# Layer 3 of a four-layer kernel: its preparation dealt out anew between the engines, and bn asked for earlier in each scan step

## The chip, the cores and the metric

The kernel runs on one core of one Trainium2 chip, as one launch. The metric is device time in microseconds (us). The kernel before was run three times; the profile is of one further execution. Engines are called as in the profile: PE (TensorE; PEld are its weight loads), DVE (VectorE), ACT (ScalarE), POOL (GpSimd) and SP (SyncE, which here issues the DMAs).

## What is computed

Four layers are applied in turn to four images of 256 channels and 64 x 64 pixels, each as x + layer(groupnorm(x)): a deformable convolution, an attention, a second deformable operation (DCNv4), and a Mamba block. Only the last is touched. With L = 4096 pixels as a sequence, 512 inner channels d and 16 states n:

```python
xz = einsum('bld,ed->ble', xs, in_proj_w);  u, res = split(xz, 2)
u = silu(depthwise_conv(u, conv_w, taps=4, causal) + conv_b)
dt, B, C = split(einsum('bld,ed->ble', u, x_proj_w), [16, 32])
delta = softplus(einsum('blr,dr->bld', dt, dt_proj_w) + dt_proj_b)
state[l] = exp(delta[l] * A) * state[l-1] + delta[l] * B[l] * u[l]     # for each d and n, along l
y[l] = sum over n of state[l] * C[l]
out = einsum('ble,de->bld', (y + u * D) * silu(res), out_proj_w)
```

## The kernel before: staging, order and names

The four images go one after the other, each through the layers 0 to 3. Layer 3 (`layer3`, L1081) cuts the 4096 pixels into 8 chunks of 512 columns. The 512 inner channels are four blocks of 128 partitions, called `dc` in the code. For each chunk the 16 states are 16 *steps*, so an image has 128 steps, s = 16 j + n for chunk j and state n.

**One step** (the loop at the end of `layer3`): DVE forms h = du * bn for four blocks (L1537). `bn` is row n of B, spread over all partitions by a matmul with `pick` (`state`, L1460), in a PSUM pool of one bank. For the states in `helped` (14, 15, 0 to 5) DVE forms only three blocks, and POOL the fourth from a row that a DMA has spread (`quarter`, L1468, `bs`). Then four scans: ACT makes da = exp(delta * A) into one of two PSUM banks (L1547), DVE runs the recurrence (L1548). Scans 0 and 1 come ahead of the middle of the step, scans 2 and 3 after it. POOL saves the last column (L1560) and multiplies by C (L1563, `cn`, also spread by a DMA). PE adds h into the four `y` banks two steps later (`add`, L1438; in a chunk's first add also u * D, L1436). At n=2 DVE multiplies the previous chunk's y by silu(res) (`gated`, L1514).

**The front.** While chunk j-1 is scanned, chunk j is prepared in *slots* of these steps, written out by hand in `front(j)`: each entry has a step, a half (0 between scans 1 and 2, 1 after scan 3, -1 and 2 at the start and the end of the step), a PE part and a rest. In order: normalise x (`begin`), four projections (L1242), four convolutions, each of four tap matmuls with diagonal weights (L1285), silu of u and of the previous chunk's gates between two table loads (`silu`, L1299, L1258), the projection to dt, B and C (`shares` L1309, `keep` L1313, and its DMA to `cd`), dt to delta (`step`, L1324, L1330, L1331), softplus in six wide operations of ACT and POOL (L1337 to L1357), the cast of B into two bf16 parts (`split`, L1369 to L1377) and four gate projections. A front's step 0 lies `LEAD` = 4 steps ahead of its predecessor's n=0 (2 for j=1). `close(j)` projects the finished chunk back and adds x (L1396, L1400), in two groups, and issues the output DMA; `fetch` loads the next image's x into the columns that became free, `count` takes its statistics on DVE (L152).

All front matmuls share one PSUM bank, so each waits until ACT has copied the one before. `fill(s, half)` issues the first PE part of a slot ahead of time, `empty` the rests. The order of the engines' queues is the order of these calls (a manual schedule): on PE in step s the part of (s,1), then `state(s + 1)`, the y adds of step s-2 and the part of (s+1,0).

**Chunk 0** has no predecessor: `first` (L1130) prepares it, and part of chunk 1, ahead of the loop. It projects four blocks (L1152). Blocks 1 and 3 are convolved by DVE (L1159, L1161), blocks 0 and 2 by PE (L1177). POOL normalises chunk 1 (L1169) and casts `pick` (L1110). After the silus (L1178, L1179), the projection (L1181), its copy `dbc` (L1184) and the dt matmuls (L1190) come the first three projections of chunk 1 and the four gate projections (L1198), and then a softplus block by block: Abs, Exp, Relu and Ln on ACT (L1220, L1221, L1222, L1215), four operations on DVE (L1223, L1224, L1216, L1217), and one subtraction (L1227) and the cast of B (L1209, L1211, L1212) on POOL. `state(0)` follows `first`; slot (0,0) then holds the fourth projection of chunk 1, and slots (0,0) and (1,0) the copies of the gates (L1492).

Of the kernel before, what the change touches and what calls it, by code (L numbers as in the profile page):

```python
# [16 lines left out]
P = 128  # L17
# [46 lines left out]
class Net:  # L64
# [1016 lines left out]
    def layer3(self, x, out, nxt, early):  # L1081
# [5 lines left out]

        nc, tc = self.nc, self.tc
        C = 512
        NC, LEAD = N // C, 4  # L1090
        with (
# [18 lines left out]
            nc.gpsimd.tensor_copy(pick.rearrange("p n m -> p (n m)"), rows.rearrange("p a b -> p (a b)"))  # L1110
# [9 lines left out]
            kept = pa.tile([P, 2, C], F32, tag="kept", name="kept")  # L1120
# [9 lines left out]
            def first():  # L1130
# [23 lines left out]
                for dc in range(4):  # L1154
                    pu = spare()
                    project(pu, xn, dc)
                    if dc % 2:
                        nc.vector.tensor_copy(up[:, dc, 3:], pu)
                        nc.vector.tensor_scalar_mul(u[:, dc, :], up[:, dc, :C], cw[:, dc, 0:1])  # L1159
                        for i in range(1, 4):  # L1160
                            nc.vector.scalar_tensor_tensor(  # L1161
                                u[:, dc, :], up[:, dc, i : i + C], cw[:, dc, i : i + 1], u[:, dc, :], ALU.mult, ALU.add
                            )
                    else:
                        nc.scalar.copy(up[:, dc, 3:], pu)
                for ct in range(2):
                    if ct == 0:
                        c1["xn"] = pa.tile([P, 2, C], F32, tag="xn3", name="xn3")
                    nc.gpsimd.tensor_scalar(  # L1169
                        c1["xn"][:, ct, :], x[:, ct, C : 2 * C], rs[:, ct : ct + 1], shift[:, ct : ct + 1], ALU.mult, ALU.add  # L1170
                    )
                nc.gpsimd.tensor_copy(tail, up[:, :, C : C + 3])
                px = bank()
                for dc in (0, 2):
                    cv = spare()
                    for i in range(4):
                        nc.tensor.matmul(cv, conv[:, dc, i, :], up[:, dc, i : i + C], start=(i == 0), stop=(i == 3))  # L1177
                    nc.scalar.activation(u[:, dc + 1, :], u[:, dc + 1, :], AF.Silu, bias=cb[:, dc + 1 : dc + 2])  # L1178
                    nc.scalar.activation(u[:, dc, :], cv, AF.Silu, bias=cb[:, dc : dc + 1])  # L1179
                for k, dc in enumerate((1, 3, 0, 2)):  # L1180
                    nc.tensor.matmul(px, xpw[:, dc, :], u[:, dc, :], start=(k == 0), stop=(k == 3))  # L1181
# [17 lines left out]

                c["gates"] = [spare() for _ in range(4)]  # L1200
                for dc, pg in enumerate(c["gates"]):
                    project(pg, xn, 4 + dc)
# [5 lines left out]
                def split(lo, hi):  # L1208
                    nc.gpsimd.tensor_copy(bp[lo:hi], dbc[lo:hi])  # L1209
                    if hi < P:  # L1210
                        nc.gpsimd.tensor_copy(t[hi:], dbc[hi:])  # L1211
                        nc.gpsimd.tensor_sub(dbc[hi:], dbc[hi:], t[hi:])  # L1212

                def end(dc):
                    nc.scalar.activation(w[:, dc, :], w[:, dc, :], AF.Ln)  # L1215
                    nc.vector.tensor_add(delta[:, dc, :], delta[:, dc, :], w[:, dc, :])  # L1216
                    nc.vector.tensor_mul(du[:, dc, :], delta[:, dc, :], u[:, dc, :])  # L1217

                for dc in range(4):
                    nc.scalar.activation(w[:, dc, :], pzs[dc], AF.Abs, bias=dtb[:, dc : dc + 1])  # L1220
                    nc.scalar.activation(du[:, dc, :], w[:, dc, :], AF.Exp, scale=-1.0)  # L1221
                    nc.scalar.activation(delta[:, dc, :], pzs[dc], AF.Relu, bias=dtb[:, dc : dc + 1])  # L1222
                    nc.vector.tensor_scalar_add(w[:, dc, :], du[:, dc, :], 1.0)  # L1223
                    nc.vector.scalar_tensor_tensor(  # L1224
                        du[:, dc, :], w[:, dc, :], -1.0, du[:, dc, :], ALU.add, ALU.subtract
                    )
                    nc.gpsimd.tensor_sub(delta[:, dc, :], delta[:, dc, :], du[:, dc, :])  # L1227
                    if dc < 3:
                        split(*((0, 64), (64, 96), (96, 128))[dc])
                    if dc:  # L1230
                        end(dc - 1)
                end(3)
                for dc in range(3):
                    nc.scalar.copy(c1["up"][:, dc, 3:], pus[dc])

# [24 lines left out]
            def front(j):  # L1260
# [17 lines left out]
                for dc in range(4):  # L1278
                    put((dc + 1) // 2, (dc + 1) % 2, *project(j, dc, lambda dc=dc: c["up"][:, dc, 3:]))

                def convolve(dc):
# [7 lines left out]
                    def rest():  # L1289
                        nc.scalar.activation(c["u"][:, dc, :], c["b"], AF.Identity, bias=cb[:, dc : dc + 1])  # L1290
                        if dc == 0:
                            nc.gpsimd.tensor_copy(tail, c["up"][:, :, C : C + 3])
# [3 lines left out]
                for dc in range(4):  # L1296
                    put(2 + dc, 1, *convolve(dc))
# [5 lines left out]
                put(6, 0, None, silu)  # L1303
# [14 lines left out]
                put(7, 1, shares, keep)  # L1318
# [16 lines left out]
                for dc in range(4):  # L1335
                    put(8 + dc // 2, dc % 2, *step(dc))
                put(10, 0, None, lambda: nc.scalar.activation(c["du"], c["du"], AF.Exp, scale=-1.0))  # L1337

                def one():
                    c["w"] = pa.tile([P, 4, C], F32, tag="w3", name="w3")  # L1340
                    nc.scalar.activation(c["w"], c["du"], AF.Identity, bias=self.ones[:, 0:1])

                put(10, 1, None, one)


                put(10, 2, None, lambda: nc.gpsimd.tensor_add(c["delta"], c["delta"], c["du"]))
                put(
                    12,
                    0,
                    None,  # L1350
                    lambda: nc.scalar.activation(c["du"], c["w"], AF.Identity, bias=self.ones[:, 0:1], scale=-1.0),
                )
                put(13, 0, None, lambda: nc.scalar.activation(c["w"], c["w"], AF.Ln))
                last = 17 if j > 1 else 15
                put(13, 2, None, lambda: nc.gpsimd.tensor_add(c["delta"], c["delta"], c["du"]))
                put((13 + last) // 2, 2, None, lambda: nc.gpsimd.tensor_add(c["delta"], c["delta"], c["w"]))
                put(last, 2, None, lambda: nc.gpsimd.tensor_mul(c["du"], c["delta"], c["u"]))  # L1357

                for dc in range(4):
                    at = ((14, 0), (14, 1), (15, 0), (15, 1)) if j > 1 else ((10, 1), (11, 0), (11, 1), (12, 1))  # L1360
                    put(*at[dc], *gate(j, dc))
# [19 lines left out]
                for i in range(3):  # L1381
                    put((11, 12, 14)[i], i % 2, None, split(i))
                return todo

            def close(j):
# [5 lines left out]
                def project(ot):  # L1391
                    def pe():
# [6 lines left out]
                        xs = kept[:, ot, :] if last else x[:, ot, bass.ts(j, C)]  # L1399
                        nc.tensor.matmul(c["b"], self.ident, xs, start=False, stop=True)  # L1400

                    def rest():
                        to = kept if last else x[:, :, bass.ts(j, C)]
# [5 lines left out]
                for ot in range(2):  # L1409
                    todo.append((11 + 2 * ot - LEAD, 1, *project(ot)))  # L1410
                if not last:
                    todo.append((15 - LEAD, -1, None, lambda: fetch(j)))

                    todo.append((13 - LEAD + DS if j < NC - 2 else 17 - LEAD, -1, None, lambda: count(j)))
# [12 lines left out]
            def keep():  # L1427
                for ct in range(2):
# [33 lines left out]
            def quarter(s):  # L1462

                if s < NC * DS:
                    c = chunks[s // DS]
                    hs[s] = pb.tile([P, 4, C], F32, tag="h", name="h", bufs=4)
                    if s % DS in helped:
                        nc.gpsimd.tensor_mul(hs[s][:, 3:4, :], c["du"][:, 3:4, :], c.pop(("bs", s % DS)))  # L1468


            slots = {}
            for j in range(1, NC):
                for step, half, pe, rest in front(j):
                    at = DS * (j - 1) - (LEAD if j > 1 else 2) + step
# [10 lines left out]
            for i in range(2):  # L1485
# [8 lines left out]
                slots.setdefault((i, 0), []).append((None, gates))  # L1494

# [20 lines left out]
            with tc.manual_schedule(  # L1516
# [10 lines left out]
                state(0)  # L1527
# [4 lines left out]
                for s in range(total):  # L1532
                    j, n = s // DS, s % DS
                    c = chunks[j]
                    h = hs.pop(s)
                    d = 3 if n in helped else 4
                    nc.vector.tensor_mul(  # L1537
                        h[:, :d, :], c["du"][:, :d, :], c.pop(("bn", n)).to_broadcast([P, d, C])
                    )
# [5 lines left out]
                    def scan(dc):  # L1545
                        da = pda.tile([P, C], F32, tag="da", name="da")
                        nc.scalar.activation(da, c["delta"][:, dc, :], AF.Exp, scale=al[:, dc, n : n + 1])  # L1547
                        nc.vector.tensor_tensor_scan(  # L1548
                            h[:, dc, :], da, h[:, dc, :], carry[:, dc, n : n + 1], ALU.mult, ALU.add
# [4 lines left out]
                    quarter(s + 1)  # L1554
                    empty(s, 0)
# [12 lines left out]
                    state(s + 1)  # L1568
# [134 lines left out]
```

## Time and profile before

| | us |
|---|---|
| median of three runs (lowest, highest) | 9831.43 (9831.18, 9837.31) |
| the profiled execution | 9825.3 |
| its span, first to last instruction | 9823.5 |
| busy in the span: PE, DVE, ACT, POOL | 8552.6, 7522.1, 4893.9, 7112.0 |
| image 0, layer 3: `shift` known | 1523.0 |
| first product, second product | 1563.7, 1570.2 |
| product of step 16 | 1683.0 |
| last scan ends | 2500.1 |

The other images begin layer 3 at 3963.8, 6388.5 and 8824.5 and take 40.5 to 41.7 from `shift` to the first product and 928 to 937 from there to the last scan's end. From the product to the last scan of image 0 the costliest groups are the scans (L1548, 512 of them, 617.3 busy), POOL's product with C (L1563, 127 that were recorded, 574.9), the y adds (L1438, 471.2), da (L1547, 346.9) and the product (L1537, 255.7).

A row of the timeline has the start, the duration from the first to the last of the merged instructions, the engine, the line, the operation with the program's names (output, then inputs), the shape, the count, and in brackets how long the engine had been idle and what ended that. A row of the waits has the total, the number of waits and the longest. A float32 matmul counts as two passes of PE, so four matmuls stand as x8.

### The profile page before, as it was taken

Reading aid. Unit: us, or ns where it says so; the run is one execution under the profiler, and the core shown is the slowest. Engines: PE = TensorE matmul, PEld = TensorE weight load, DVE = VectorE, ACT = ScalarE, POOL = GpSimd, SP = SyncE. Lnnn points to the kernel's source line nnn. Section 1 sums busy time; section 2 is a strip of 40 time slices with the busy share of each in tenths; the row PEclk is TensorE's granted clock in tenths of the full one; section 3 lists DMA queues with packets and bytes.
Section 4 is the critical chain, followed back from the end, with each engine's and each line's share of the span. In section 5 each row is a group of like instructions: output and inputs, shape, how many; then the busy total and the mean of one; then the engine's idle time right before and its main releaser. Section 6 shows DMA issues by size and latency. Waiting matters only on the chain. (4 is left out here: it accounts for less than half of the span.)

```text
span 9823.5 us, 89566 instructions
## 1 busy us (share of the span) xinstructions
PE 8552.6 (87%) x29129; PEld 4208.7 (43%) x29129; DVE 7522.1 (77%) x8175; ACT 4893.9 (50%) x7532; POOL 7112.0 (72%) x4220
## 2 busy tenths in 40 slices
PE   5789998998778999899878899989987889998997
PEld 3643343333464344333346434433334643443333
DVE  4764498999676459899968645989996764689998
ACT  3753335665474333566547433266655733326664
POOL 3746687888474668798857467789985746778997
PEclk9999999999899999999989999999998999999999
DMA  7840011222783001122279201122228820111221
GB/s 255 319 158 1 26 50 56 64 62 67 257 320 139 1 30 47 58 63 63 67 272 333 107 1 35 51 57 62 62 64 313 324 73 1 39 51 55 60 60 51
DMA packets 415274, 1024.78 MB, mean 104 GB/s; under 512 B 38771, under 2 KB 111916, under 8 KB 412748
## 3 DMA queue, kind: packets, MB, share of 16 engines
q0 software_dynamic: 165888, 604.05, 17.0%
q1 hardware_dynamic: 248908, 414.90, 13.7%
q8 instruction: 233, 3.82, 0.2%
q14 instruction: 245, 2.01, 0.1%
HBM read 851.70 MB, written 93.37 MB: 96 GB/s over the span
## 5 line engine op out<-in xcount | busy, mean ns | idle before, releaser
L1548 DVE TENSOR_TENSOR_SCAN h<-da,carry,h 128x512 f32<-128x512 f32 x2048 | 2469.0, 1264 | 138.3 <-ACT da L1547 78.0
L1563 POOL TENSOR_TENSOR h<-h,cn 128x2048 f32<-128x2048 f32 x508 | 2299.7, 4527 | 41.3 <-POOL carry L1560 0.8
L1547 ACT ACTIVATE da<-delta,l3a 128x512 f32<-128x512 f32 x2048 | 1393.1, 689 | 1064.1 <-DVE h L1548 1061.5
L1438 PE MATMUL y<-h,ident 128*128 128x512 f32 x4096 | 1907.6, 610 | 12.4 <-POOL h L1563 12.4
L344 POOL DMA_INDIRECT g<-tab,idx x1152 | 1359.8, 1180 | 748.6 <-issue 367.5
L565 POOL TENSOR_TENSOR acc<-acc,e 128x1024 f32<-128x1024 f32 x480 | 1126.0, 2346 | 539.5 <-ACT e L561 517.6
L388 PE MATMUL pz<-cols,l0w 128*128 128x256 f32 x4608 | 1211.3, 409 | 184.6 <-DVE cols L377 73.9
L1438 PEld LDWEIGHTS y<-h,ident 128*128 128x128 f32 x4096 | 801.7, 196 | 1251.6 <-issue 1166.7
L353 DVE SCALAR_TENSOR_TENSOR r<-g,wx,r 128x512 f32<-128x512 f32 x1152 | 858.4, 745 | 373.4 <-ACT r L352 251.4
L462 DVE TENSOR_REDUCE m<-pm 128x3 f32<-128x1536 f32 (+2 forms) x340 | 599.5, 1763 | 699.9 <-PE pm L452 699.9
L1537 DVE TENSOR_TENSOR h<-du,bn 128x2048 f32<-128x2048 f32 (+1 forms) x512 | 1022.8, 1998 | 49.9 <-PE bn L1460 49.8
L388 PEld LDWEIGHTS pz<-cols,l0w 128*128 128x128 f32 x4608 | 893.2, 204 | 353.7 <-DVE cols L377 110.4
L561 ACT ACTIVATE e<-sc 128x1024 f32<-128x1024 f32 x512 | 496.1, 1020 | 1029.5 <-PE sc L548 1029.5
L572 PE MATMUL cx<-e,v 128*128 128x512 f32 x2048 | 1001.0, 616 | 0.0
L845 DVE TENSOR_TENSOR prod<-ring,A 128x1280 f32<-128x1280 f32 x640 | 922.4, 1480 | 77.9 <-DMA ring<-ring 60.2
L352 ACT ACTIVATE r<-g,wx 128x512 f32<-128x512 f32 x1152 | 826.5, 717 | 265.0 <-DMA g<-tab,idx 211.6
L862 PE MATMUL pacc<-prod,ident 128*128 128x512 f32 x1920 | 914.5, 611 | 32.8 <-DVE prod L845 21.8
L854 POOL TENSOR_TENSOR prod<-prod 128x512 f32<-128x512 f32 x640 | 801.2, 1277 | 182.2 <-DVE prod L845 157.3
L370 PE MATMUL pt<-ident,acc 128*128 128x128 f32 x2304 | 428.3, 293 | 295.0 <-DVE acc L361 234.2
L572 PEld LDWEIGHTS cx<-e,v 128*128 128x128 f32 x2048 | 352.4, 189 | 599.3 <-issue 596.8
L360 ACT ACTIVATE acc<-r,wy 128x256 f32<-128x256 f32 x1152 | 571.3, 496 | 16.5 <-DVE r L353 13.7
L361 DVE SCALAR_TENSOR_TENSOR acc<-r,wy,acc 128x256 f32<-128x256 f32 x1152 | 548.6, 477 | 0.0
(255 smaller groups left out, 10767.4 us busy)
## 6 DMA issues: line engine op xcount, KB each, us to landing
cn<-cd SPq DMA_DIRECT2D x512, 256.0 KB
tab<-vt SPq DMA_DIRECT2D x112, 640.0 KB
bs<-cd SPq DMA_DIRECT2D x256, 256.0 KB
ring<-ring SPq DMA_DIRECT2D x288, 126.0 KB
ring<-ring SPq DMA_DIRECT2D x288, 124.0 KB
g<-tab,idx POOLq DMA_INDIRECT x1152
x<-in_x SPq DMA_DIRECT2D x64, 256.0 KB
out<-x SPq DMA_DIRECT2D x56, 256.0 KB
```

Source lines behind the costliest of these rows:

```text
L344: nc.gpsimd.indirect_dma_start(out=g[:], out_offset=None, in_=tab[:, :], in_offset=bass.IndirectOffsetOnAxis(ap=idx[:, t, k : k + 1], axis=0),
L353: nc.vector.scalar_tensor_tensor(r, g[:, :, 1, :], wx[:, 1, t, k : k + 1], r, ALU.mult, ALU.add)
L388: nc.tensor.matmul(sums[m][:, ot, :256], wf[:, i, bass.ts(ot, P)], cols[m][:, i, :], start=(i == 0), stop=(i == 17),)
L565: nc.gpsimd.tensor_add(b["acc"], b["acc"], e)
L572: nc.tensor.matmul(blocks[qb]["cx"], v[:, 4 * (i + kt // 4 * 4) + kt % 4, :], e[:, bass.ts(i % 2, 512)], start=(kt == 0 and i == 0), stop= ...
L845: nc.vector.tensor_mul(d["prod"][:, :, t, :].rearrange("p x (g c) -> p x g c", c=GC), ring[y // VR % 4][:, :, y % VR, :].rearrange("p x (g ...
L862: nc.tensor.matmul(d["pd"], self.ident, prod[:, wx, :], start=(wy == 0 and wx == 4), stop=(wy == WIN - 1 and wx == 2),)
L1438: nc.tensor.matmul(c["ys"][dc], self.ident, h[:, dc, :], start=False, stop=(n == DS - 1))
L1537: nc.vector.tensor_mul(h[:, :d, :], c["du"][:, :d, :], c.pop(("bn", n)).to_broadcast([P, d, C]))
L1547: nc.scalar.activation(da, c["delta"][:, dc, :], AF.Exp, scale=al[:, dc, n : n + 1])
L1548: nc.vector.tensor_tensor_scan(h[:, dc, :], da, h[:, dc, :], carry[:, dc, n : n + 1], ALU.mult, ALU.add)
L1563: nc.gpsimd.tensor_mul(h, h, cn.to_broadcast([P, 4, C]))
```

## The change

All of it lies in `layer3`. `first`: blocks go in the order 1, 3, 0, 2; DVE convolves 1, 3 and 0, PE only 2; the cast of `pick` and the normalisation of chunk 1 move from POOL to ACT, as do the casts of B (the subtraction between them stays on POOL), each a block later; Relu and Ln write back into the PSUM bank, and DVE makes the subtraction that POOL had. `state(0)` and then the gate projections stand at the end of `first`.

The loop: `state(s + 1)` moves to the middle of the step, ahead of `fill(s, 1)`. `product` is a function; in the steps of `visits` (those with silu and table loads) the product of the next step is issued in the middle of the step. POOL's quarter has a tile of its own, `hq`. Within a slot the entries with a PE part go first.

The slots: `LEAD` is 5 (3 for j=1). As seen from the scan, with j > 1: projections 0 to 2 and convolutions 0 and 1 come one step earlier, projection 3 one step and a half later, and convolutions 2 and 3 stay; the silus, `keep` and dt stay; the casts of B go to n=6, 7 and 10 and Exp stays at n=6, the two wide Identity operations to the first half of n=7 and the second half of n=8, Ln to the second half of n=9, the gates to n=9 and 10; `close` to n=6 and 8 (from 7 and 9), `fetch` to n=10, and `count` from n=9 to the middle of n=2 of the same chunk. Slot (0,0) holds the first convolution of chunk 1. `kept` shares the buffer of `xn3`.

```diff
-        NC, LEAD = N // C, 4
+        NC, LEAD = N // C, 5
...
-                for dc in range(4):
+                c1["xn"] = pa.tile([P, 2, C], F32, tag="xn3", name="xn3")
+                for dc in (1, 3, 0, 2):
                     pu = spare()
                     project(pu, xn, dc)
-                    if dc % 2:
+                    if dc == 1:
                         nc.vector.tensor_copy(up[:, dc, 3:], pu)
+                    else:
+                        nc.scalar.copy(up[:, dc, 3:], pu)
+                    if dc != 2:
                         nc.vector.tensor_scalar_mul(u[:, dc, :], up[:, dc, :C], cw[:, dc, 0:1])
...
+                    if dc == 3:
+                        nc.scalar.copy(pick.rearrange("p n m -> p (n m)"), rows.rearrange("p a b -> p (a b)"))
...
-                c["gates"] = [spare() for _ in range(4)]
-                for dc, pg in enumerate(c["gates"]):
-                    project(pg, xn, 4 + dc)
...
                 def split(lo, hi):
-                    nc.gpsimd.tensor_copy(bp[lo:hi], dbc[lo:hi])
+                    nc.scalar.copy(bp[lo:hi], dbc[lo:hi])
                     if hi < P:
-                        nc.gpsimd.tensor_copy(t[hi:], dbc[hi:])
+                        nc.scalar.copy(t[hi:], dbc[hi:])
                         nc.gpsimd.tensor_sub(dbc[hi:], dbc[hi:], t[hi:])
                 def end(dc):
-                    nc.scalar.activation(w[:, dc, :], w[:, dc, :], AF.Ln)
-                    nc.vector.tensor_add(delta[:, dc, :], delta[:, dc, :], w[:, dc, :])
+                    nc.scalar.activation(pzs[dc], w[:, dc, :], AF.Ln)
+                    nc.vector.tensor_add(delta[:, dc, :], pzs[dc], delta[:, dc, :])
...
-                    nc.gpsimd.tensor_sub(delta[:, dc, :], delta[:, dc, :], du[:, dc, :])
-                    if dc < 3:
-                        split(*((0, 64), (64, 96), (96, 128))[dc])
+                    nc.vector.tensor_sub(delta[:, dc, :], pzs[dc], du[:, dc, :])
                     if dc:
                         end(dc - 1)
+                        split(*((0, 64), (64, 96), (96, 128))[dc - 1])
                 end(3)
                 for dc in range(3):
                     nc.scalar.copy(c1["up"][:, dc, 3:], pus[dc])
+                state(0)
+                c["gates"] = [spare() for _ in range(4)]
+                for dc, pg in enumerate(c["gates"]):
+                    project(pg, xn, 4 + dc)
...
-                    put((dc + 1) // 2, (dc + 1) % 2, *project(j, dc, lambda dc=dc: c["up"][:, dc, 3:]))
+                    at = ((0, 1), (1, 0), (1, 1), (4, 1))[dc]
+                    put(*at, *project(j, dc, lambda dc=dc: c["up"][:, dc, 3:]))
...
-                    put(2 + dc, 1, *convolve(dc))
+                    at = ((2, 1) if j > 1 else (3, 0), (3, 1), (5, 1), (6, 1))[dc]
+                    put(*at, *convolve(dc))
...
-                    todo.append((11 + 2 * ot - LEAD, 1, *project(ot)))
+                    todo.append((6 + 2 * ot, 1, *project(ot)))
...
+            def product(s):
+                if s not in hs:
+                    c, n = chunks[s // DS], s % DS
+                    h = hs[s] = pb.tile([P, 4, C], F32, tag="h", name="h", bufs=4)
+                    d = 3 if n in helped else 4
+                    nc.vector.tensor_mul(h[:, :d, :], c["du"][:, :d, :], c.pop(("bn", n)).to_broadcast([P, d, C]))
...
+            for todo in slots.values():
+                todo.sort(key=lambda part: part[0] is None)
...
                     scan(0)
                     scan(1)
                     quarter(s + 1)
+                    state(s + 1)
+                    if s in visits:
+                        product(s + 1)
                     empty(s, 0)
                     fill(s, 1)
                     scan(2)
                     scan(3)
                     empty(s, 1)
...
                     empty(s, 2)
-                    state(s + 1)
                     late.append((j, n, h))
```

## The prediction, made before the changed kernel ran

> **What bounds the kernel now.** I read the page's busy shares first, then the table by stage of the first image's layer 3, then VectorE's waits there, then the timeline of single steps. Times are microseconds of the profiled execution; a step is one pass of the scan loop, D is the start of its product (L1537), n its number within a chunk of 16.
>
> The stage table (length, busy time of PE, PEld, DVE, ACT, POOL, clock) of the preparation, of chunk 0 and of one later chunk:
>
> ```profile
> 1522.98:1563.67 40.69, 37.19 (x81) 15.68 (x81) 26.37 (x30) 19.43 (x31) 24.11 (x30) 0.95 0.12 41
> 1563.67:1683.00 119.33, 100.43 (x230) 41.85 (x231) 108.19 (x82) 75.92 (x106) 97.54 (x47) 0.99 0.16 47
> ...
> 1821.68:1939.18 117.50, 107.17 (x254) 45.70 (x253) 111.55 (x87) 74.25 (x103) 105.49 (x48) 1.00 0.22 62
> ```
>
> A chunk of 117.5 is VectorE's (111.6 busy), but TensorE has 107.2 and GpSimd 105.5: three engines within 10% of the end. Whatever holds one of them back a few us is seen. VectorE's waits in this layer (total, times, longest):
>
> ```profile
> DVE h L1548 <- ACT da L1547: 19.6, 16, 4.4
> DVE h L1537 <- PE bn L1460: 12.3, 22, 1.0
> ...
> DVE h L1548 <- POOL h L1468: 2.6, 1, 2.6
> ```
>
> From step 16 on (1683 to 2500) the same view has 14.1 for da and 10.9 for bn: 25.0 an image. The first is the silu visit at n=2 (two table loads, two 2048-wide silus, 6.32 from the first load to the next da), the second TensorE's conv steps, 7.09 against VectorE's 6.56.
>
> The timeline of step 0 shows how close behind the preparation the rest stands:
>
> ```profile
> 1559.66 0.38 PE L1460 MATMUL bn<-bp,pickn 128*128 128x512 bf16 x1 [0.21 <-POOL bp L1209]
> ...
> 1561.34 1.98 PE L1242 MATMUL front<-xn,l3a 128*128 128x512 f32 x4 [1.31 <-ACT up L1234]
> ...
> 1563.38 0.60 ACT L1246 COPY up<-front 128x512 f32<-128x512 f32 x1
> 1563.67 1.75 DVE L1537 TENSOR_TENSOR h<-du,bn 128x1536 f32<-128x1536 f32 x1
> ...
> 1570.24 1.73 DVE L1537 TENSOR_TENSOR h<-du,bn 128x1536 f32<-128x1536 f32 x1
> ```
>
> The gates (L1198) are through before the first bn, and TensorE has only one small projection (L1242) before ScalarE's da for scan(2). Two steps on, a conv of the front starts 0.9 before the step's product, and a close of two groups takes 4.3:
>
> ```profile
> 1575.91 3.70 PE L1285 MATMUL front<-up,conv 128*128 128x512 f32 x8 [2.63 <-ACT u L1290]
> ...
> 1576.80 1.73 DVE L1537 TENSOR_TENSOR h<-du,bn 128x1536 f32<-128x1536 f32 x1
> ...
> 1849.68 3.60 PE L1396 MATMUL front<-sres,l3b 128*128 128x512 f32 x8
> ...
> 1853.11 1.02 PE L1400 MATMUL front<-x,ident 128*128 128x512 f32 x2
> 1853.97 0.38 PE L1460 MATMUL bn<-bp,pickn 128*128 128x512 bf16 x1
> ```
>
> So TensorE works ahead of VectorE today: the lead, not its speed, keeps ScalarE's copies, and the da behind them, on time.
>
> **What the Trainium skill says.** "TensorE: Matmul & The Clock Gate", section "What's actually happening": the array falls to half clock after an idle window of about 3.4 us, windows running free. The trace agrees: after idles of 4.20 and 2.83 at 1519 to 1524 the passes of L1152 come 0.85 apart, later 0.43; after idles of 2.4 within a chunk it happened about every second time, and after those of 3.28 in the last chunks each time, for 3 to 7 passes. The same page, "Architectural detail": ScalarE and VectorE are strict FIFO; so a copy that waits holds every da behind it. "SBUF — State Buffer", "SBUF: two separate sides": a VectorE operation with two SBUF inputs and a GpSimd one lock each other out; L1217 takes 0.69 alone and 1.53 beside GpSimd. "ScalarE: Activation LUTs", "What ACT_TABLE_LOAD costs": 1283 ns; here 1.28, and no drain to be seen after it.
>
> **The change, part by part.**
>
> *Preparation.* VectorE's first convolution waits for the head of up, which GpSimd writes at 1529.39 (0.20). Three of 2.84 each (1535.47 to 1538.31, undisturbed, since GpSimd has lost the pick cast and the normalisation) end at 1538.1. TensorE's one convolution, 8 passes of 0.43 on a copy that ends at 1533.4, ends at 1537.0. ScalarE's added work (pick cast 1.9, by a 2048-wide row; one more copy 0.59; normalisation 2 x 0.65) and its load end at 1535.9: beside it. Silus in order end at 1539.0, the last pass of L1181 at 1540.4 instead of 1543.0. So the first Abs comes 2.6 earlier, at 1542.3. ScalarE then has, up to the third split copy, four triples of 1.82, three Ln of 0.52 and five casts of about 0.6: 11.9, so bp is whole at 1554.2. VectorE takes the four subtractions (L1514, also with one input in PSUM, has 0.68). Not seen before are an activation that writes PSUM and a 2048-wide cast on ScalarE: between nothing and 0.1 more for each of eight, and 1.9 (GpSimd's own cast) to 2.0 (L1341); I take nothing and 1.9. First product about 1557.9, 5.8 earlier than 1563.67.
>
> But state(0) now stands ahead of the gates on TensorE, which is in order too. From 1554.2: bn 0.2; gates 16 x 0.43 = 6.9; conv 0 of chunk 1, now in slot (0,0) where the small projection was, 8 x 0.43 + 0.16 = 3.6: 1564.95. Behind that in ScalarE's queue: the conv's copy 0.6, two gate copies 1.1, da(2) 0.7. scan(2) of step 0 starts at 1567.3, though VectorE could at 1562.1. Two scans (2.35) and the second product stands at 1569.65, against 1570.24: only 0.6 remains of 5.8. And TensorE idles from 1549.7 to 1554.2, so the gates start cold: 4.5 passes x 0.42 = 1.9 (0 to 3). **+1.3 an image.**
>
> *Steps 1 to 5.* state(s+1) moves ahead of fill(s,1), and bn has one bank, so TensorE waits for product(s) (D+1.8) before each step's work. Queued behind that wait are fill(s,1), the y passes of s-2 and fill(s+1,0); ScalarE's copies of the two fills wait for these, and da behind the copies. After: conv from D2+2.05 3.44, diag and y 6.88, bn 0.22, conv 3.6: D2+16.2; copy and da 1.3: scan(0) of step 4 at D2+17.5, which VectorE could do at 15.0. Two da 1.2 more, the silu block 6.32, da 0.7: scan(2) at D2+25.0; the product of step 5, moved into this hole, is free; scan(0) of step 5 at D2+27.45. Before: 1603.32-1576.80 = 26.52. +0.9, and the conv of step 2 after an idle of 4.5: +1.7 (0 to 3). **+2.6.**
>
> *Steps 6 to 16.* At step 9 the slot's gate goes first (the sort) and ends on TensorE at D+2.47; then copy 0.48, casts 1.22, L1341's row 1.91, da 0.7: scan(2) at D+6.8, natural 4.8. 2.0 against 0.58 before: +1.5. Step 12, projection late: +0.3. From step 12 GpSimd's three wide adds and the product set step 15 before and after; they pass the delay on. **+1.8.**
>
> *Six later chunks.* Removed: the 25.0. product(s+1) (1.75) and, in three images, the statistics (1.28) fill the visit's 2.2; bn is early. Added, by the same walk, where an undisturbed step is 7.09 and scan(0) and scan(2) stand at D+2.37 and D+4.78. n=6: close starts at D+2.5 behind bn and ends 4.5 later, 0.1 before D7. Copy 0.48, two da 1.22, two casts 1.25, L1341 1.90, da 0.70: scan(2) at D7+5.46, **0.68** late. n=8: close again; copy 0.48, L1351 1.91, da 0.70: scan(0) at D9+3.0, **0.63** late. TensorE goes on from close with y 3.43 and gate 1.72+0.16, to D9+5.04; copy and da 1.2: scan(2) at D9+6.25, with the first delay in it still **0.84** late. Then gate (bank free 0.6 later), y, gate, to D10+4.16; copy, cast, da 1.8: scan(2) at D10+5.97, **1.19** late. At the conv steps (n=13 to 1) a copy ends by D+6.8 and the next scan(0) is at D+8.4: nothing. GpSimd's product reaches n=15 about 0.2 late (0 to 0.5). Sum 3.54. At n=8 TensorE idles 3.3 before close: cold passes cost 0 to 2.0, I take 1.0. 6 x 4.54 = 27.2, less 25.0: **+2.2.**
>
> *At nothing:* kept in xn3's buffer (its readers are through at n=10 of chunk 6); hq for h (GpSimd's waits there were 0.9 in all); fetch, out and cd on SP, moved a step at most (their 0.3 to 0.4 issues lie ahead of cn loads wanted two steps later; one step, 6.6, if not). The last chunk has no front: 0.
>
> Sum +1.3 +2.6 +1.8 +2.2 = +7.9 an image, four images +31.6. On the profiled execution (9825.3, span 9823.5) 9856.9; on the median of the runs, 9831.4, which is 6.1 more, **9863**.
>
> **Rivals.** (a) *The cold clock doesn't bite.* Prologue -0.6, +0.9, +1.8, chunks 6 x 3.54 - 25.0 = -3.8: -1.7 an image, 9825. For it: half of the 2.4 idles left no mark. Against: those of 3.3 did. (b) *The covers pay*, the other side: TensorE's slack (10 us a chunk) is enough to be on time at n=7 to 10, no new wait appears, 25.0 go; with the first chunk even, 100 in all: 9731; half of it 9781. It decides at close: if those passes end before D+6.0, where ScalarE's third and fourth da are through, nothing is late. Against: ten passes of 0.43 can't start before D+2.5. (c) *TensorE becomes the bound*: cold at both ends of each chunk, 2 more a chunk: 9910.
>
> **How the numbers follow.** Forecast 0.55 (its own range 9846 to 9900), (a) 0.25, (b) 0.14, (c) 0.06. The range 9812 to 9900 leaves out (b) and (c). 0.2% is 19.7 us, about what a measurement of this kernel can tell from no change: faster 0.15, same 0.25, slower 0.60.
>
> **What would show it.** The first product 5 to 6 earlier than 40.7 after shift, but the second one not; in step 0 a da wait of 5 to 8 behind the conv's copy; bn waits of VectorE near zero; the da wait at n=2 gone in the later chunks and new ones of about 0.7, 0.6, 0.8 and 1.2 at n=7, 9, 9 and 10; passes 0.85 apart at the gates and at close. Wrong if the second product comes before 1567, or if da waits from step 16 on are below 10 an image.

## The result, and the profile after

The changed kernel takes 9892.7 us (median of six runs, 9873.2 to 9910.9), the kernel before beside it 9835.0: a ratio of 1.0058, interval 1.0045 to 1.0071. Measured once more beside the experiments it is 1.0042 (1.0028 to 1.0056). It is slower, by nearly twice the forecast's 31.6 us in the first pair (57.7) and by about as much as that in the second (33.6).

The profiled execution took 9885.6 us (span 9883.7), 60.2 more in span than that of before. Layers 0 to 2 hold 13.9 of these (by image -5.5, +7.5, +16.0, -4.1). The change doesn't touch them, and with the same code they take 1404 to 1477 us for each of the last three images from one run's trace to another's, so I count layer 3 alone: it agrees within 0.2 between the two traces of the changed kernel (after and after_again, the same kernel once more). Its marks, mean of the four images, in us after `shift` is known (e9_warm_ready and the other labels are the experiments below):

| kernel | first product | second product | step 5, scan(0) | step 16, scan(0) | last scan's end | from step 16 to the end |
|---|---|---|---|---|---|---|
| before | 40.9 | 47.5 | 81.0 | 162.5 | 975.4 | 812.9 |
| after | 35.6 | 49.5 | 85.5 | 168.5 | 987.0 | 818.6 |
| after_again | 35.7 | 49.9 | 86.7 | 169.6 | 986.9 | 817.2 |
| e1_bn_late | 35.6 | 49.8 | 81.9 | 163.7 | 950.4 | 786.8 |
| e8_no_cover | 36.1 | 50.3 | 83.3 | 165.9 | 956.6 | 790.7 |
| e6_best | 35.8 | 44.7 | 79.6 | 161.9 | 948.6 | 786.7 |
| e2_before_bn_early | 41.1 | 47.8 | 84.0 | 168.0 | 1015.0 | 847.1 |
| e5_before_cover | 41.1 | 47.7 | 79.8 | 161.3 | 968.0 | 806.7 |
| e3_gates_behind_conv | 35.5 | 47.7 | 86.9 | 169.8 | 988.9 | 819.1 |
| e9_warm_ready | 35.2 | 49.1 | 85.8 | 168.7 | 980.7 | 812.0 |

Layer 3 of after is 11.6 longer than before, an image, and 46.5 in all, where the forecast had 31.6. The stage table of after, image 0 (preparation, chunk 0, and one later chunk of 16 steps, about two steps earlier in the scan than the one shown for before), shows where:

```profile
1517.52:1552.49 34.97, 28.05 (x57) 11.69 (x58) 23.35 (x36) 25.08 (x38) 9.31 (x18) 0.89 0.17 47
1552.49:1684.00 131.51, 112.15 (x250) 47.23 (x249) 108.07 (x82) 76.57 (x108) 97.43 (x46) 0.95 0.15 43
1801.68:1918.15 116.47, 107.10 (x254) 45.88 (x253) 111.32 (x87) 73.99 (x102) 105.36 (x49) 1.00 0.21 64
```

The preparation has lost 5.7, chunk 0 has gained 12.2 at the same busy time of VectorE (108.07 against 108.19): it is all waiting. The later chunk is 1.0 shorter, but it is one of those that ran warm; others of this image take up to 119.3. VectorE's waits in this layer (total, times, longest):

```profile
DVE h L1563 <- ACT da L1561: 48.7, 33, 7.1
DVE h L1563 <- POOL hq L1473: 3.8, 1, 3.8
DVE h L1481 <- PE bn L1466: 1.0, 1, 1.0
```

So the bn waits are gone (12.3 to 1.0) and the da waits have gone from 19.6 to 48.7. Over all images, VectorE's waits for da, bn and GpSimd are in before 9.9 an image up to step 16 and 24.7 from there on; in after 21.5 and 31.6. The first of the new da waits, in the timeline of step 0:

```profile
1549.36 0.58 PE L1466 MATMUL bn<-bp,pickn 128*128 128x512 bf16 x1 [4.55 <-ACT bp L1203]
1549.74 8.43 PE L1151 MATMUL front<-xn,l3a 128*128 128x512 f32 x16
...
1558.01 3.60 PE L1285 MATMUL front<-up,conv 128*128 128x512 f32 x8
...
1563.17 1.32 ACT L1561 ACTIVATE da<-delta,l3a 128x512 f32<-128x512 f32 x2
1563.92 1.28 DVE L1563 TENSOR_TENSOR_SCAN h<-da,carry,h 128x512 f32<-128x512 f32 x1 [7.12 <-ACT da L1561]
...
1566.30 1.73 DVE L1481 TENSOR_TENSOR h<-du,bn 128x1536 f32<-128x1536 f32 x1
```

The gates stand behind bn and ahead of the convolution; ScalarE waits for that convolution, and its third da is behind it. The conv of step 2, which began 0.9 before the step's product, now begins 2.15 after it (1575.01 against 1572.86), since the bn ahead of it waited 4.46 for that product:

```profile
1572.86 1.73 DVE L1481 TENSOR_TENSOR h<-du,bn 128x1536 f32<-128x1536 f32 x1
...
1574.63 0.59 PE L1466 MATMUL bn<-bp,pickn 128*128 128x512 bf16 x1 [4.46 <-DVE h L1481]
```

The same in a later chunk, at n=8: bn, the close, ScalarE's copy, its wide row, da, and the scan of n=9 that comes late:

```profile
1742.98 2.26 DVE L1481 TENSOR_TENSOR h<-du,bn 128x2048 f32<-128x2048 f32 x1
...
1745.30 0.38 PE L1466 MATMUL bn<-bp,pickn 128*128 128x512 bf16 x1 [3.35 <-DVE h L1481]
...
1745.51 3.59 PE L1401 MATMUL front<-sres,l3b 128*128 128x512 f32 x8
...
1748.94 1.02 PE L1405 MATMUL front<-x,ident 128*128 128x512 f32 x2
...
1750.00 0.59 ACT L1409 COPY x<-front 128x512 f32<-128x512 f32 x1 [1.47 <-PE front L1405]
...
1750.48 2.01 ACT L1376 ACTIVATE du<-w,ones 128x2048 f32<-128x2048 f32 x1
...
1752.39 1.29 ACT L1561 ACTIVATE da<-delta,l3a 128x512 f32<-128x512 f32 x2
1753.11 2.46 DVE L1563 TENSOR_TENSOR_SCAN h<-da,carry,h 128x512 f32<-128x512 f32 x2 [0.78 <-ACT da L1561]
```

The bracket on bn names the wait: TensorE stood idle for 3.35 with the close behind it, until VectorE's product had read the only bank. Three chunks later the same idle time ends at half clock (the granted clock is 0.50 from 2096 to 2099): eight passes take 6.38 instead of 3.59, and the wait is 3.73.

```profile
2096.13 0.59 PE L1466 MATMUL bn<-bp,pickn 128*128 128x512 bf16 x1 [3.35 <-DVE h L1481]
...
2096.51 6.38 PE L1401 MATMUL front<-sres,l3b 128*128 128x512 f32 x8
...
2106.89 1.28 DVE L1563 TENSOR_TENSOR_SCAN h<-da,carry,h 128x512 f32<-128x512 f32 x1 [3.73 <-ACT da L1561]
```

### The profile page after: what moved, and what is told of

Same layout as the page of the kernel before. It is cut to its first block, busy times and chain, and to the rows that moved or that the text cites. A ratio compares the mean times of both kernels' runs of the same rounds, so it can differ in the third digit from the quotient of the medians.

```text
span 9883.7 us, 89236 instructions
## 1 busy us (share of the span) xinstructions
PE 8576.0 (87%) x29097; PEld 4228.8 (43%) x29097; DVE 7505.6 (76%) x8203; ACT 4907.8 (50%) x7568; POOL 7040.4 (71%) x4172
## 5 line engine op out<-in xcount | busy, mean ns | idle before, releaser
L1563 DVE TENSOR_TENSOR_SCAN h<-da,carry,h 128x512 f32<-128x512 f32 x1792 | 2173.1, 1265 | 239.2 <-ACT da L1561 193.0
L1444 PE MATMUL y<-h,ident 128*128 128x512 f32 x4096 | 1878.3, 602 | 10.5 <-POOL h L1581 10.5
L388 PE MATMUL pz<-cols,l0w 128*128 128x256 f32 x4608 | 1227.0, 413 | 183.2 <-issue 86.7
```

The costliest lines, as they stand in the source:

```text
L388: nc.tensor.matmul(sums[m][:, ot, :256], wf[:, i, bass.ts(ot, P)], cols[m][:, i, :], start=(i == 0), stop=(i == 17),)
L1444: nc.tensor.matmul(c["ys"][dc], self.ident, h[:, dc, :], start=False, stop=(n == DS - 1))
L1563: nc.vector.tensor_tensor_scan(h[:, dc, :], da, hb, carry[:, dc, n : n + 1], ALU.mult, ALU.add)
```

## The experiments

The theory after the result: the place of `state(s + 1)`, ahead of the shares that TensorE has in the middle of the step, makes the kernel slower; the rest of the change makes it faster. Rivals: the lost lead comes from the new slots themselves; the prologue's order sets it all; the cold clock sets it all.

**e1_bn_late** puts the state back to the end of the step, except in the visits. Nothing else is moved.

```diff
                     quarter(s + 1)
-                    state(s + 1)
                     if s in visits:
+                        state(s + 1)
                         product(s + 1)
...
                     empty(s, 2)
+                    if s not in visits:
+                        state(s + 1)
```

> The changed kernel with bn of the next step asked for at the end of the step, as before, except in the steps of visits. Theory A (TensorE lost its lead because bn stands ahead of the front's matmuls): the da waits at n=7, 9 and 10 (0.81, 0.78 or more, 0.80, 1.38) go or fall below 0.3, bn waits of VectorE come back with 5 to 12 us an image, the stretch from step 16 to step 114 falls from 726 to about 708 an image, the time to 9805 to 9840. Theory B (the half slots of ScalarE are too full, wherever bn stands): the same waits stay at n=7 to 10, 9880 to 9895. Theory C (only the cold clock hurts): the 0.8 and 1.38 waits stay, 9860 to 9880.

Measured: 9542.2 us, ratio to before 0.9874 (0.9854 to 0.9895). Layer 3 is 36.6 an image shorter than in after and 25.0 shorter than in before. VectorE's waits, and the same n=8:

```profile
DVE h L1563 <- ACT da L1561: 13.9, 5, 7.8
```
```profile
1695.29 3.60 PE L1401 MATMUL front<-sres,l3b 128*128 128x512 f32 x8
...
1698.72 1.02 PE L1405 MATMUL front<-x,ident 128*128 128x512 f32 x2
1699.58 0.38 PE L1466 MATMUL bn<-bp,pickn 128*128 128x512 bf16 x1
```
```profile
1696.27 2.26 DVE L1481 TENSOR_TENSOR h<-du,bn 128x2048 f32<-128x2048 f32 x1
```

The product of this step starts at 1696.27: the close begins 1.0 before it, in after 2.5 behind it. From step 16 on 0.7 of da waits are left of 31.6, and the bn waits do not come back. Theory A had the direction, but not the size: the stretch from step 16 to the third scan of step 114, forecast at 708, is 694.9, for the most part because the 5 to 12 of bn waits that were to return did not. So the early bn costs 36.6 an image here, and it is not what took the bn waits away.

**e2_before_bn_early** makes that one move in the kernel before.

```diff
                     quarter(s + 1)
+                    state(s + 1)
...
                     empty(s, 2)
-                    state(s + 1)
```

> The kernel before with one line moved: bn of the next step in the middle of the step, ahead of the front's matmul. Theory A: the 12.3 us of bn waits an image fall below 2, but da waits of 0.5 to 2 appear in the steps with a close or gates (n=8 to 11), and the waits at steps 3 to 5 of chunk 0 grow by 2 to 3; 9845 to 9890. Theory B: with the old slots nothing new waits, and the bn waits are gained: 9785 to 9800.

Measured: 9806.7, ratio 1.0154 (1.0133 to 1.0174); layer 3 is 39.6 an image longer. In image 0 the bn waits vanish (no line of them is left) and the da waits go from 19.6 to 65.8:

```profile
DVE h L1548 <- ACT da L1547: 65.8, 55, 5.2
```

That is theory A's direction and more than its size: its upper end, 9890, is 1.006 of the kernel before. The da waits stand above all at n=2, 4 and 10, about 1.5 to 2.5 each. In both kernels, then, the move has the same sign and nearly the same size (36.6 and 39.6), with the old slots and with the new. In before it does remove its 12.3 of bn waits, and pays 46 for them.

**e5_before_cover** adds only the cover to the kernel before: in the eight steps with silu and table loads (4, 18, 34 and every 16th up to 114), state and product of the next step are issued in the middle, so that VectorE has work while ScalarE's da is late.

```diff
+            visits = [4] + [DS * j + 2 for j in range(1, NC)]
...
+                    if s in visits:
+                        state(s + 1)
+                        product(s + 1)
...
-                    state(s + 1)
+                    if s not in visits:
+                        state(s + 1)
```

> The kernel before with only the cover: in the steps with silu and table loads bn and the product of the next step are issued in the middle of the step. Theory A: the product of 1.75 fills the hole, the da waits at these steps fall from 4.4, 1.4 and five of 2.2 to about 2.7, 0 and 0.5, some 12 us an image: 9780 to 9795. Rival (the early bn costs TensorE's lead even in these eight steps, or the moved product delays the scans): 9820 to 9845.

Measured: 9627.1, ratio 0.9969 (0.9954 to 0.9984); layer 3 7.4 an image shorter. The da waits from step 16 on go from 14.0 to 8.0; the bn waits stay as they were, at 10.6. So the cover is worth less than the 12 that theory A expected.

**e8_no_cover** takes the cover out of e1_bn_late (out of the steps named under e5_before_cover; the 36, 54 and so on of the expectation below are a slip), so that of the change the slots and the preparation remain.

```diff
-                    if s in visits:
-                        state(s + 1)
-                        product(s + 1)
...
-                    if s not in visits:
-                        state(s + 1)
+                    state(s + 1)
```

> e1_bn_late without its visits: no product is put ahead of a scan any more in steps 4, 18, 36, 54, 72, 90 and so on, and every state is asked for at the end of its step; the slots of the preparation stay as the change has them. It tells how much of the 25 us an image that e1_bn_late gains on the kernel before lies in the cover and how much in the slots. My estimate, from the wait of 2.2 us at n = 2 in each of six chunks that the cover hides in the kernel before (e5_before_cover: 7.4 an image): layer 3 is 7 to 12 us an image longer than in e1_bn_late (ratio to the kernel before 0.990 to 0.992). Rival: in the new slots nothing is late at n = 2 and the cover is idle: then the ratio stays at 0.987.

Measured: 9581.3, ratio 0.9922 (0.9904 to 0.9939); layer 3 6.2 an image longer than e1_bn_late and 18.8 shorter than before. From step 16 on VectorE waits 3.9 for da and nothing for bn, against 24.7 in all in before. The slots alone, which here stand for all of the change but the cover and the early bn (the sort and `hq` were not tried apart), remove the bn waits and most of the da waits; what the cover still adds is 2.2 up to step 16 and 4.0 behind it, a little less than I had estimated.

**e3_gates_behind_conv** moves the four gate projections of the first chunk behind the first convolution, and their copies one step on.

```diff
-                c["gates"] = [spare() for _ in range(4)]
-                for dc, pg in enumerate(c["gates"]):
-                    project(pg, xn, 4 + dc)
+                def gates():
+                    c["gates"] = [spare() for _ in range(4)]
+                    for dc, pg in enumerate(c["gates"]):
+                        project(pg, xn, 4 + dc)
...
-                slots.setdefault((i, 0), []).append((None, gates))
+                slots.setdefault((i + 1, 0), []).append((None, gates))
...
                 fill(0, 0)
+                gate_mms()
```

> The changed kernel with the gate projections of chunk 0 issued behind the first convolution of chunk 1 instead of ahead of it, and their copies one step later. If the da wait of 7.2 in step 0 is TensorE's queue (theory A): it falls below 1, the second product comes 5 to 7 sooner (about 43 after shift instead of 49.5), and step 16 too, since the step that GpSimd sets is only shifted: 9865 to 9875. Rival: GpSimd or the later convolutions set steps 3 to 15 by themselves, and the gain is given back by step 16: 9885 to 9895.

Measured: 9696.4, ratio 1.0039 (1.0026 to 1.0052). A miss: the wait of step 0 falls from 7.2 to between 1.75 and 2.45, but the gates now stand ahead of state(1), and the second product comes at 47.7, not at 43; step 1 waits 3.3 for bn and 3.0 for da. By step 5 layer 3 is 1.4 later than in after, and at its end 1.9: the gain is given back, as the rival had it, though by the bn and da waits of step 1 rather than later. The 16 passes have to go somewhere where nobody waits.

**e6_best** is e1_bn_late with these passes dealt two projections by two behind the shares of steps 0 and 1, with state(1) and state(2) in the middle of their steps.

```diff
-                    if s in visits:
+                    if s in visits or s < 2:
                         state(s + 1)
...
                     fill(s, 1)
+                    if s < 2:
+                        gate_mms(2 * s, 2 * s + 2)
```

> The changed kernel with the states of the last experiment but at the end of the step (as in e1_bn_late, states ahead only in the visits and in steps 0 and 1), and the four gate projections of the first chunk dealt two by two behind the shares of steps 0 and 1, their copies behind those of step 1. My theory: TensorE's gate passes ahead of the first convolution are what ScalarE's first da copies wait behind. Then the wait of 7.1 us before the second scan goes, the second product is at 42 to 43 us after the shift instead of 49.8, and layer 3 is 6 to 7 us an image shorter than e1_bn_late (ratio to the kernel before 0.984 to 0.985). Rival: the gain is given back by step 15, which the copies and GpSimd's sums set, as it was in e3_gates_behind_conv: then the step 16 marker is where e1_bn_late has it, 163.6, and the ratio stays at 0.987.

Measured: 9533.7, ratio 0.9873 (0.9855 to 0.9890), the same as e1_bn_late within the intervals. The step-0 wait is 2.3 and the second product comes 5.1 earlier; at the mark of step 16 1.8 is left, and at the end as much. Step 4 takes back most of it (its bn wait is 3.7 in every image, in e1_bn_late 0.3 in two and 2.0 in two), and the steps up to 15 another 0.5. The rival held in the main, though not to the point: the mark is 161.9, not 163.6.

**e7_warm** gives TensorE three products in after, at the end of each step n=7, so that it isn't idle before the close.

```diff
                     fill(s + 1, 0)
+                    if j and n == 7:
+                        warm = bank()
+                        for dc in range(3):
+                            nc.tensor.matmul(warm, self.ident, h[:, dc, :], start=True, stop=True)
```

> The changed kernel plus three extra fp32 products into a spare bank (their result is never read) at the end of every step with n = 7 of chunks 1 to 6, so that TensorE isn't idle before the close at n = 8. It adds work and leaves none out. If the lower granted clock at the close is what makes the first wait of n = 9 vary between 0.8 and 3.7 us, that wait is 0.8 in every chunk now, and the stretch from step 16 to step 114 is 5 to 8 us an image shorter than the changed kernel's 726.4. Rival: the wait comes from the order of the queues and not from the clock: then it stays as it is, and the stretch is the same or up to 6 us longer by the added passes (6 passes of about 0.3 us in each of 6 chunks).

Measured: 9941.1, ratio 1.0290 (1.0271 to 1.0309), and neither theory's number. The edit has a fault of its own: the products read the step's own h, which GpSimd was still multiplying by C.

```profile
1702.66 4.48 PE L1593 MATMUL front<-h,ident 128*128 128x512 f32 x6 [8.65 <-POOL h L1581]
1706.98 0.38 PE L1466 MATMUL bn<-bp,pickn 128*128 128x512 bf16 x1
```

They wait 8.65, start cold (4.48 for six passes, where about 0.3 each had been expected), and bn behind them makes VectorE wait 5.25, and da 5.14 more. The stretch from step 16 to step 114 is 780.0, 55 more than in after_again, from three products a chunk that nobody needed. It is the same as with bn: the matmul at the head of TensorE's queue waited, here 8.65, and the matmuls behind it waited with it.

**e9_warm_ready** mends it: the products read constant diagonals.

```diff
-                            nc.tensor.matmul(warm, self.ident, h[:, dc, :], start=True, stop=True)
+                            nc.tensor.matmul(warm, self.ident, conv[:, dc, :, :].rearrange("p a b -> p (a b)"), start=True, stop=True)
```

> e7_warm once more with its fault mended: the three extra fp32 products at the end of each step with n = 7 of chunks 1 to 6 read the convolution's constant diagonals, which are always there, where e7_warm's read a tile that GpSimd still held, so that the next state stood behind them. They are never read and leave nothing out. In the changed kernel TensorE idles 3.35 us before the state that is followed by the close. If the lower granted clock after that idle time makes the first wait of n = 9 vary between 0.4 and 3.7 us, it is 0.4 to 0.8 in every chunk now, and the stretch from step 16 to step 114 is 5 to 8 us an image shorter than the 724.8 of after_again. Rival: six passes of 0.43 us don't keep the clock up, or the wait isn't the clock's: then the waits and the stretch stay within 2 us of after_again.

Measured: 9893.0, ratio 1.0017 (1.0009 to 1.0024). The step that was cold above:

```profile
2091.09 2.74 PE L1593 MATMUL front<-conv,ident 128*128 128x512 f32 x6
2094.60 0.38 PE L1466 MATMUL bn<-bp,pickn 128*128 128x512 bf16 x1 [0.77 <-DVE h L1481]
2094.82 3.60 PE L1401 MATMUL front<-sres,l3b 128*128 128x512 f32 x8
```

The first wait of n=9 is 0.77 in 22 of 24 chunks and 0.42 in two. In after it is over 1 in 14 of 24 (2.06 to 3.74), mean 1.82 against 0.74 here. The stretch from step 16 to step 114 is 719.6: 6.8 an image shorter than in after (726.4) and 5.2 shorter than in after_again. More work for TensorE made the kernel faster. But the waits at n=7, 9 and 10 stay, 0.7 to 1.4 each, with every close warm; so the cold clock at the close is about a sixth of the 36.6 (6.3 at the last scan's end). The rest isn't the clock's either: by the clock records of the traces, TensorE is at half clock for 10.1 us an image between step 16 and the last chunk here, in before for 13.7 and in after for 22.5.

**e10_two_banks** and **e11_one_bank** were to test the bank directly: after with two PSUM banks for bn against after with one, in both with da in SBUF (to free the bank), cn in three buffers and hq in one. The two differ in the last line only.

```diff
-                        da = pda.tile([P, C], F32, tag="da", name="da")
+                        da = pb.tile([P, C], F32, tag="das", name="da")
...
-            self.banks(2, "l3d") as pda,
-            self.banks(1, "l3b") as pbb,
+            self.banks(1, "l3d") as pda,
+            self.banks(2, "l3b") as pbb,
```

> The changed kernel with two PSUM banks for the broadcast row bn instead of one. The bank is taken from da, whose two buffers lie in SBUF here; to make room there cn has three buffers instead of four and hq one instead of two. To be compared with e11_one_bank, which has the same da, cn and hq and one bank for bn. My theory of the 36.6 us an image by which the changed kernel's layer 3 is longer than that of e1_bn_late: a state in the middle of the step waits for the only bank until VectorE's product of the same step has read it, and whatever TensorE has queued behind it (shares of the preparation, the close, y) comes later by that. With a second bank nothing waits there: 20 to 36 us an image shorter than e11_one_bank, the waits of da at n = 7, 9 and 10 gone. Rival: it isn't the bank but the order of TensorE's work: then the two kernels agree within 5 us an image.

> The control of e10_two_banks: the changed kernel with da in SBUF, cn in three buffers and hq in one, and bn in one PSUM bank as it was. If these moves cost nothing, layer 3 is at 985 to 989 us after the shift as in the changed kernel; the single hq buffer may add waits for GpSimd at n = 15 to 5, up to some 10 us an image, which e10_two_banks has too.

Measured: 11867.2 and 11864.1, ratios 1.2016 (1.1990 to 1.2042) and 1.2013 (1.1988 to 1.2038). Inconclusive on what a second bank saves: they agree within 0.4 an image, but layer 3 is at 1475 us after `shift`, not at 985 to 989, since VectorE's scans have become so slow that TensorE is early in both. On what bn waits for the pair does tell: with one bank TensorE stands idle ahead of bn until the product has read the bank, 387 times and for 1770.5 us in all; with two, 65 times and for 137.9. First e10_two_banks, then e11_one_bank (total, times, longest):

```profile
PE bn L1466 <- DVE h L1481: 137.9, 65, 5.7
```
```profile
PE bn L1466 <- DVE h L1481: 1770.5, 387, 11.1
```

The scan's group (line, shapes, count, busy time, mean ns) in after and in e11_one_bank:

```profile
L1563 DVE TENSOR_TENSOR_SCAN h<-da,carry,h 128x512 f32<-128x512 f32 x1792 | 2173.1, 1265 | 239.2 <-ACT da L1561 193.0 <-DVE h L1481 2.7
```
```profile
L1563 DVE TENSOR_TENSOR_SCAN h<-da,carry,h 128x512 f32<-128x512 f32 x1792 | 4148.9, 2369 | 94.2 <-ACT da L1561 47.6 <-DVE h L1481 2.3
```

## Why the prediction was right, and where it was wrong

The side, the places and the mechanism were right; 9892.7 lies in the range, 29.7 above the forecast. Layer 3 alone is 46.5 longer in the four images, half as much again as the forecast 31.6; in after_again it is as much longer (11.5 an image). That the measured differences, 57.7 and 33.6, lie on either side of this comes from layers 0 to 2, whose time varies and which the forecast left alone, so the nearness of the second to the forecast is luck. By its steps:

- *Preparation*, forecast +1.3: measured +2.0. The first product is 5.3 earlier (forecast 5.8), the second later. In image 0, the forecast's walk with the cold gates (1569.65 + 1.9, less the 5.46 by which `shift` is earlier) gives 1566.1; it was 1566.30, the wait 7.12. The gates took 8.43, of which 1.5 over 16 x 0.43 is the clock. By the letter one sign of being wrong came true, "if the second product comes before 1567"; it had not allowed for an earlier `shift`, and counted from `shift` the second product is later, as forecast.
- *Steps 1 to 5*, forecast +2.6: measured +2.5. Against e1_bn_late, early bn costs 4.0 there (from the second product to step 5: 36.0, e1_bn_late 32.0, before 33.5); cover and slots give back 1.5. The conv of step 2 was cold, as assumed: in image 0 its first six passes start 0.85 apart.
- *Steps 6 to 16*, forecast +1.8: measured +1.5. Step 9 waits 2.19 (forecast 2.0).
- *Six later chunks*, forecast +2.2: this is the term that was too small. The added waits stand at the places named: n=7 0.81 (forecast 0.68), n=9 0.78 where it is warm, and 0.80 (0.63, 0.84), n=10 1.37 (1.19). The cold close costs 1.82 - 0.74 = 1.1 a chunk (1.0). Not foreseen were 0.3 to 1.4 at n=1 and 0.8 at n=2 of the first of these chunks and about 0.4 at n=7 of the last; the 0.2 a chunk for GpSimd at n=15 did not come. In all 31.6 of da waits, where 27.2 were added up. The 24.7 of before are gone, as counted. By these waits the term is +6.9; by the marks it is +5.7 (818.6 against 812.9). Nearly all of the difference is in VectorE's busy time, which is 776.5 an image in this stretch against 777.6 in before.

What was wrong is a cause, not a number: "bn is early" stood among what removes the 25.0, and its price among what is added, as if the two came together. e1_bn_late and e8_no_cover part them. The slots remove the waits: from step 16 on 24.7 fall to 3.9 with no cover and no early bn, and the cover takes most of the rest. The early bn removes nothing that the slots have not removed, and brings nearly all of the 31.6 (0.7 are left without it). So the change is a gain of 25.0 an image and a loss of 36.6; I had the sum nearly right, without seeing that it came apart along one line of code.

Rival (b), the covers pay, is therefore what the same change does without that move. It said 9731 for 25.0 an image, deciding "if those passes end before D+6.0"; in e1_bn_late they end at 1699.7, D+3.5, because the close need not wait for the product, and the ratio 0.9874 on 9831 is 9708. Rival (a), no cold clock, is e9_warm_ready from step 16 on: 812.0 against 812.9 in before (the rival had -3.8). The cold clock did bite, in 14 of 24 chunks. The Trainium skill's "TensorE: Matmul & The Clock Gate", section "What's actually happening", puts the fall to half clock after an idle window of about 3.4 us; here idle times of 3.35, all alike, ended cold 14 times and warm 10 times, and in before those of 2.4 at n=8 were followed by passes 0.85 apart 9 times in 24 (the prediction read "about every second time"). So in this case an idle time shorter than that window is at times enough. Rival (c) did not occur in its size: it had 12 an image more in the six later chunks than the forecast, and the marks have 3.5 more.

Open: whether a second bank for bn would save the early state. The experiment for it was spoilt by its own way of freeing the bank. That the bank is what holds bn is read from the brackets of the trace (bn released by the product's reading), and the same pair bears it out, since TensorE's idle time ahead of bn falls from 1770.5 to 137.9 with the second bank; that the 36.6 would go with it is not shown.

## What to carry to other kernels

An operation that is issued earlier still runs only when what it waits for is there; in this case it held back those behind it in its engine's queue until then. Before moving one ahead, read its release in the timeline, and what stands between the old place and the new: here one matmul of 0.38 us with a wait of 3.35 was put ahead of passes on which ScalarE's da depended. When a change has several parts, price each part against the others undone, since a gain of 25 and a loss of 37 look from outside like a small loss.

## What the runs showed of the hardware

In e11_one_bank the scan, with da in SBUF, is 1.25 us while GpSimd is idle (1220 scans) and 3.83 in the mean while GpSimd runs beside it (828 scans, up to 5.55); in after, with da in PSUM, it is 1.26 in either case. The Trainium skill names a reason ("SBUF — State Buffer", section "SBUF: two separate sides": a VectorE operation with two SBUF inputs and a GpSimd operation that reads SBUF lock each other out), and this case agrees, its times being those above: the place of one operand makes the group of scans 1976 us longer (4148.9 against 2173.1).

In e9_warm_ready six needless passes of 0.46 us, put into an idle time of 3.35 (which leaves 0.77), save 1.1 us each chunk: no close is cold, where 14 of 24 were.
